# Decoder layer on one core: sixteen W2 product banks and eleven transposes moved from ScalarE to VectorE, and norms laid in other places

## The chip, the cores and the metric

The kernel runs on one core of a Trainium2 chip. The metric is the device time of one execution in microseconds (us), and a kernel is told by the median of several runs. The engines are TensorE (PE, with its weight loads PEld), VectorE (DVE), ScalarE (ACT), GpSimd (POOL) and SyncE (SP), which issues most transfers. Each engine works through its own instructions in a fixed order; an instruction that waits for another engine holds up all that stand behind it.

## The reference

One decoder layer in float32 on x of 16 x 112 x 512 (1792 tokens), with a context of 16 x 375 x 512 and its mask. D = 512, 16 heads of 32, a hidden width of 2048:

```python
x = x + self_attention(layernorm(x))        # q, k, v low-rank: Wdown, Wup fold into the weights
x = x + cross_attention(layernorm(x), ctx, mask)
      # clip(scores) -> softmax -> @ v -> Wo + bo; delta = rs * that;
      # delta is normalised again, times ln_gamma plus ln_beta
x = x + ffn(layernorm(x))
      # hidden = silu(x W1^T) * (x W3^T); hidden = fwht(hidden); hidden @ W2^T
```

The Hadamard transform `fwht` of the hidden vector (2048 wide, over sqrt(2048)) is applied by the kernel to W2 instead.

## The kernel before, in words

The 1792 tokens are 14 tiles of 128 rows (`xr`) and also 16 batches of 112 tokens; 4 batches make a group. `xyT` holds the tokens transposed, as input of every projection. PSUM has three banks named `mm`, which projections, transposes and W2 products share in turn; `sc` (two pairs of banks) takes scores and transposes of the exponentials; `ys` takes the weighted values.

**PE's order is written out by hand.** Every piece of PE work that has slack is a generator that yields the microseconds it took, and `Filler` draws from a queue of such pieces between the steps of attention: `fill(us)` draws that much, `drain()` the rest. `mixed(a, b, skip)` draws `skip` pieces from `a` and then one of each in turn. A new piece takes the `mm` bank that comes free first; its matmuls wait for the copy that empties that bank. The other engines' instructions are ordered by a scheduler, around the instruction that `tc.issue_after` names.

**Start.** The layer norm of the first tiles (`n1[0]`), the folded weights (`fold`, L849 to L857), the first group's queries and keys. Then `attention.begin` puts out the first scores, and behind them the fold of wv is mixed with the transposes of `n1[1]` (L1622 to L1625).

**Self attention** goes through 16 lays, one for each batch. Lay b (`SelfAttention.step`, L1002) first issues the scores of batch b + 1: on DVE two maxima (L981) and their scaling (L982), then on ACT 16 exponentials (L986), 8 for each half; then on DVE sum, reciprocal and multiply for each half (L997 to L999). While these run, PE fills with the lay's pieces: queries or keys of the next group (L865, copied out of PSUM by ACT at L871), values (L883, copied at L888), transposes of normalised tiles (L826, copied by ACT at L827), W2 products, or the output projection (L894). Then PE transposes the exponentials of batch b (L1019, copied by ACT at L1021) and multiplies them with the values (L921).

**W2** is transformed in two parts. In lays 0 to 3 PE multiplies it with a Hadamard matrix, four products a lay (L1539), and ACT copies each bank back with a factor (L1542). From lay 1 on, `w2_steps` does the rest on DVE and ACT: subtraction and addition (L1569, L1570) and a copy (L1571), 4 or 5 steps a lay (`prepared`), put behind the lay's last multiply. Its last steps store blocks to DRAM from row buffers; rows of one kind (`row`) share four buffers with `xn`.

**Norms.** `Norm.start` does statistics (L766, L767), a reciprocal root by 12 small instructions (`rstd_of`, L774 to L786), and a normalised row tile `xn` for each token tile (L792). `n1` norms feed the self projections, `n2` the cross projections, `n3` the feed-forward part. Before, `n1[2]` is started ahead of lay 2, `n1[3]` ahead of lay 7, and each `n2[g]` at the end of `after_self`, the self output projection of group g, in lays 5, 9, 12 and in cross batch 0.

**Cross attention** goes through 16 batches with three key blocks each (`Cross.step`). For each block: scores, exponentials (L1244) and a check pass (L1248) on ACT, weighted values of the block before (L921), and on DVE the addition of the exponentials (L1274). At a batch's end `divide` sums over keys (L932), takes four reciprocals (L1284) and multiplies (L1285). PE fills with values, keys and queries of the next batch: values are copied by DVE (L888), the keys' sums of products are made on DVE (L1110 to L1143, and L1054 which reads the context `cT` straight from a load). In batches 3, 7 and 11 the next group's transposes are mixed with its queries. `AfterCross` does the cross output projection of a group, then its own norm and the residual (`finish`: rstd, L1202, L1210, statistics), then starts `n3`. `pieces()` runs `finish` as one burst behind the projections.

**Feed-forward** (`Pass`) follows, bound by PE.

Of the kernel before, what the change touches and what calls it, by code (L numbers as in the profile page):

```python
# [14 lines left out]
AF = mybir.ActivationFunctionType  # L15
# [3 lines left out]
P = 128  # L19
# [578 lines left out]
def finite_layer(  # L598
# [203 lines left out]
    class Norm:  # L802
# [11 lines left out]
                normalised(self.l, self.tiles, self.rstd, k) for k in range(len(self.tiles))  # L814
            ]

        def begin(self):
            self.start(True)
            yield 0.0

        def transposes(self):

            for k, t in enumerate(self.tiles):
                tr = psum("mm", [P, C, P])
                for c in range(C):
                    nc.tensor.transpose(tr[:, c, :], self.xn[k][:, ts(c, P)], ident)  # L826
                nc.scalar.copy(xyT[:, :, ts(t, P)], tr)  # L827
                yield 0.5
            if self.l == 1:

                beta = row("beta")
                nc.gpsimd.dma_start(out=beta, in_=c_beta.partition_broadcast(P))
                for t in self.tiles:
                    nc.gpsimd.tensor_tensor(xr[:, t, :], xr[:, t, :], beta, ALU.add)
# [124 lines left out]
    def after_self(tiles, norm):  # L959

        for t in tiles:
            yield from project(
                wo, t, lambda acc: nc.vector.tensor_tensor(xr[:, t, :], acc, xr[:, t, :], ALU.add)
            )
            stats(xr[:, t, :], norm.l, t)
        norm.start(False)

    class SelfAttention:


        def begin(self, b, grp):
            bl = b % GB
            scs = scores(
                lambda i, j: grp.q[ds(i * DH, DH), j, ts(bl, S)],
                lambda i, j: grp.k[ds(i * DH, DH), j, ts(bl, S)],
                S,
            )
            es = []
            for sc, (tag, bufs) in zip(scs, (("q", 2), ("es", 3))):
                mx = ln.tile([S, 2, HG], F32, tag="mx", name="mx")  # L980
                nc.vector.reduce_max(mx, sc, axis=AX.X)  # L981
                nc.vector.tensor_scalar(mx, mx, -SCALE, None, op0=ALU.mult)  # L982
                e = pair("e", tag, bufs)[:S]
                for i in range(2):
                    for j in range(HG):
                        nc.scalar.activation(  # L986
                            e[:, i, j, :],
                            sc[:, i, j, :],
                            AF.Exp,
                            scale=SCALE,  # L990
                            bias=mx[:, i, j : j + 1],
                        )
                es.append((e, mx))


            for e, total in es:
                nc.vector.reduce_sum(total, e, axis=AX.X)  # L997
                nc.vector.reciprocal(total, total)
                self.behind = nc.vector.tensor_tensor(  # L999
                    e, e, total.unsqueeze(3).to_broadcast([S, 2, HG, S]), ALU.mult  # L1000
                )
            self.next = b, grp.v, [e for e, _ in es]  # L1002
# [177 lines left out]
    class AfterCross:  # L1180
# [15 lines left out]
        def finish(self):  # L1196

            rstd = rstd_of(2, self.tiles, rs2)
            nc.vector.tensor_scalar(rstd, rstd, rs, None, op0=ALU.mult)
            for k, t in enumerate(self.tiles):  # L1200
                d = self.d[k]
                nc.vector.scalar_tensor_tensor(  # L1202
                    d,
                    in0=d,
                    scalar=mv[:, 2, t, 0:1],
                    in1=rows["gamma"],
                    op0=ALU.subtract,
                    op1=ALU.mult,
                )
                nc.vector.scalar_tensor_tensor(  # L1210
                    xr[:, t, :],
                    in0=d,
                    scalar=rstd[:, k : k + 1],
                    in1=xr[:, t, :],
                    op0=ALU.mult,
                    op1=ALU.add,
                )
                stats(xr[:, t, :], self.norm.l, t)
            self.norm.start(False)

        def pieces(self):
            yield from self.projections()
            self.finish()

    class Cross:

# [44 lines left out]
        def add(self, late, i):  # L1271
            if late is not None and late[1] > 0:
                total = self.es[i][:KP]
                nc.vector.tensor_tensor(total, total, late[3][i][:KP], ALU.add)  # L1274

        def divide(self, late):
            if late is not None and late[1] == KC - 1:
# [258 lines left out]
    def w2_products(h, w):  # L1536
        for c in range(0, UNITS, 2):
            acc = psum("mm", [P, D])
            nc.tensor.matmul(  # L1539
                acc, h, w[:, ds(c, 2)].rearrange("p c n -> p (c n)"), start=True, stop=True  # L1540
            )
            nc.scalar.activation(  # L1542
                w[:, ds(c, 2)].rearrange("p c n -> p (c n)"),
                acc,
                AF.Copy,
                scale=1.0 / math.sqrt(FF),
            )
            yield 0.9

# [50 lines left out]

    pe = ctx.enter_context(tc.manual_schedule(engines={mybir.EngineType.PE}))
    f = Filler()

    n1 = [Norm(0, r) for r in read]
    n2 = [Norm(1, r) for r in whole]
# [12 lines left out]
    f.drain()  # L1618
    n1[1].start(True)
    f.add(mixed(grp[0].keys(), block_products(1)))  # L1620
    f.drain()
    attention = SelfAttention()  # L1622
    attention.begin(0, grp[0])
    f.add(mixed(fold(wv, raws[2], bdm[1]), n1[1].transposes()), grp[0].values(range(GB)))
    f.drain()  # L1625
    w2_load()
    h = w2_matrix()
# [4 lines left out]
    def lay(b, us, *pieces, prepared=0):  # L1632
        f.add(*pieces)
        attention.step(b, grp[min(b + 1, B - 1) // GB], f, us, prepared)

    lay(0, 15.5, mixed(grp[1].queries(), w2_products(h, w2[0])))
    lay(1, 15.5, mixed(grp[1].keys(), w2_products(h, w2[1])), prepared=4)
    n1[2].start(True)
    lay(2, 14, mixed(grp[1].values(range(3)), w2_products(h, w2[2])), prepared=4)
    lay(  # L1640
        3,
        9.5,
        mixed(grp[1].values(range(3, GB)), w2_products(h, w2[3])),
        n1[2].transposes(),
        prepared=4,
    )

    lay(4, 12, grp[2].queries(), prepared=4)
    lay(5, 10.5, after_self(whole[0], n2[0]))
    lay(6, 13.5, mixed(grp[2].keys(), n2[0].transposes(), 5), prepared=5)  # L1650
    n1[3].start(True)
    lay(7, 15.5, mixed(grp[2].values(range(GB)), n1[3].transposes(), 3), prepared=5)

    lay(8, 12, grp[3].queries(), prepared=5)
    lay(9, 14, after_self(whole[1], n2[1]))
    lay(10, 14, mixed(grp[3].keys(), n2[1].transposes(), 5), prepared=5)
    for _ in w2_prep:
        pass
    xk, xv, xq, xo = (weight(n) for n in ("xk", "xv", "xq", "xo"))
# [2 lines left out]
    load_weight(xq, c_wq_t)  # L1662
    load_weight(xo, c_wo_t)
    kv.append(Keys(0))
    lay(11, 14, grp[3].values(range(GB)))

    xks = weight("xks").rearrange("p c n -> p (c n)").rearrange(
        "p (s k n) -> p s k n", s=4, k=2
# [3 lines left out]
    ]  # L1672
    s_sums(xks, *xk_blocks)
    lay(12, 10.5, after_self(whole[2], n2[2]))
    lay(13, 10, kv[0].first_keys())
    kv.append(Keys(1))
    lay(14, 12, mixed(kv[0].values(), n2[2].transposes(), 3))
    qs = [Queries(n) for n in range(B // 2)]
# [2 lines left out]
    cross = Cross()  # L1681
    n3w = None
    passes = [Pass(n) for n in range(2)]
    for b in range(B):
        g, bl = divmod(b, GB)
        us = 0.0
        if b + 2 < B:
            kv.append(Keys(b + 2))
        if b + 1 < B:
            kv[b + 1].sums()  # L1690
            us += 19.5
        if bl == 0:
            if g == 0:
                f.add(after_self(whole[3], n2[3]))
            elif g < 3:
                f.add(AfterCross(whole[g - 1], n3[g - 1]).pieces())
            us += 13.0 if g < 3 else 0.0
        if b + 1 < B:


            f.add(mixed(kv[b + 1].values(), kv[b + 1].keys(), 2))
            if b % 2:
                queries = qs[(b + 1) // 2].pieces()
                us += 6.0
                if bl == 3 and g < 3:
                    queries = mixed(queries, (n2[3] if g == 0 else n3[g - 1]).transposes())
                    us += 2.0
                f.add(queries)
        if b == B - 1:
            after = [AfterCross(whole[g], n3[g]) for g in (2, 3)]  # L1710
            f.add(after[0].projections())
            us += 10.5
        if b == B - 2:
            ready.update({(0, i): load_blocks(0, i) for i in range(2)})
        if b == B - 1:
            passes[0].token_sums()
        for kc in range(KC):
            cross.step(b, kc, qs[b // 2].q, kv[b], f, us / KC)
        f.drain()
    cross.weigh(cross.late)  # L1720
    cross.add(cross.late, 0)
# [27 lines left out]
    p.start()  # L1749
    p.products(0, 0)  # L1750
    with tc.issue_after(p.last):
        after[0].finish()
    p.products(0, 1)
    def tiles_of(pieces):

        for _ in pieces:
            next(pieces, None)
            yield

    def tiles_of(pieces):  # L1760
# [5 lines left out]
    late = itertools.chain(  # L1766
        itertools.repeat(None, 1),
        n3[2].transposes(),
        tiles_of(after[1].pieces()),
        itertools.repeat(None, 3),  # L1770
        n3[3].transposes(),
    )
# [97 lines left out]
```

## Time and profile before

| | us |
|---|---|
| runs of the kernel before: lowest, median, highest | 1395.64, 1396.09, 1397.08 |
| the profiled execution | 1396.93 |
| its span (first to last instruction) | 1395.1 |
| DVE busy, ACT busy in the span | 785.2, 470.7 |
| idle of PE at 52.53, ended by ACT's copy of wv (L857) | 3.05 |
| idle of PE at 76.94, 98.49, 121.70, 140.84, ended by ACT's W2 copy (L1542) | 1.95, 1.97, 1.53, 1.53 |
| idle of PE at 155.50 and 307.98, ended by exponentials (L986) | 1.28, 2.65 |
| idle of PE at 473.00, 609.22, 746.44, ended by ACT's copy of transposes (L827) | 1.32 each |
| idle of PE at 505.66, 645.77, ended by DVE's copy of values (L888) | 2.17, 1.09 |

Times at the left are where the idle time ends, counted from the span's start. The profile is of one execution: its own time is 1.83 us longer than its span, and 0.84 above the median of the runs. In the profile a row names line, engine and operation, the tiles written and read, and how long; `<-` in brackets names the engine and line that ended the wait ahead of it. "Granted clock" is the share of TensorE's full clock that the chip gave in a stretch of time.

### The profile page before, as it was taken

How to read it: one execution, taken by the hardware profiler on the slowest of the kernel's cores; microseconds unless marked ns; L12 is line 12 of the kernel's file. 1: busy time of each engine (PE TensorE's matmuls, PEld its weight loads, DVE VectorE, ACT ScalarE, POOL GpSimd, SP SyncE). 2: the span in 40 equal slices, each digit the busy share in tenths (PEclk: the TensorE clock that was granted, in tenths of full speed). 3: DMA queues.
4: the chain of work that ended last, by engine and by line, in shares of the span. 5: the costliest groups of instructions: out<-in, count | busy, mean ns of one | idle time of the engine just before them, and what ended most of it. 6: DMA issues, size and time to landing. Idle time of an engine off the chain costs nothing.

```text
span 1395.1 us, 20037 instructions
## 1 busy us (share of the span) xinstructions
PE 1357.1 (97%) x8328; PEld 809.2 (58%) x8328; DVE 785.2 (56%) x1493; ACT 470.7 (34%) x917; POOL 36.5 (3%) x68
## 2 busy tenths in 40 slices
PE   8989999999999999999999999999999999999997
PEld 5544555556676757666777775544555555555554
DVE  5244998773646575558554556756754235555332
ACT  3355755544244434443445355110110001111000
POOL 2000010030000100000000000000000000000000
PEclk9999999999999999999999999999999999999999
DMA  9100002421000000000000102111031112311301
GB/s 322 42 1 0 31 8 84 166 90 46 23 23 24 30 24 23 24 23 23 23 24 23 39 16 61 46 46 46 20 123 59 56 59 84 91 61 66 115 1 55
DMA packets 59719, 74.02 MB, mean 53 GB/s; under 512 B 2640, under 2 KB 47712, under 8 KB 57316
## 3 DMA queue, kind: packets, MB, share of 16 engines
q1 hardware_dynamic: 57952, 69.44, 15.0%
q0 software_dynamic: 672, 1.62, 0.4%
q8 instruction: 67, 1.10, 0.3%
q10 hardware_dynamic: 996, 1.59, 0.3%
q14 instruction: 32, 0.26, 0.1%
HBM read 61.63 MB, written 11.01 MB: 52 GB/s over the span
## 4 chain that ended last, share of the span: by engine, by line
PE 85%; DVE 9%; ACT 4%; issue 1%; DMA 1%; POOL 0%; SPq 0%; ACTq 0%; DVEq 0%; POOLq 0%
PE mm L883 13%; PE gate L1454 12%; PE mm L1096 9%; PE mm L865 8%; PE ys L1454 7%; PE mm L894 6%; PE gate L1388 6%; PE mm L1454 5%; PE sc L910 4%; PE ys L1388 3%; PE ys L921 3%; PE mm L1388 3%; ACT e L986 2%; DVE mx L981 1%; PE sc L1019 1%
## 5 line engine op out<-in xcount | busy, mean ns | idle before, releaser
L883 PE MATMUL mm<-xv,cT 128*125 128x512 f32 x384 | 180.4, 606 | 3.3 <-DVE v L888 3.3
L1244 ACT ACTIVATE e<-sc,bia,scl 125x896 f32<-125x896 f32 x64 | 68.5, 1095 | 200.3 <-PE sc L910 200.3
L883 PEld LDWEIGHTS mm<-xv,cT 128*125 128x125 f32 x384 | 68.7, 188 | 79.7 <-issue 74.7
L1248 ACT ACTIVATE sc<-sc,limit,nscl 125x896 f32<-125x896 f32 x96 | 102.7, 1070 | 0.0
L1454 PE MATMUL gate<-t,f 128*128 128x448 f32 x256 | 101.4, 539 | 0.0
L1274 DVE TENSOR_TENSOR es<-es,e 125x896 f32<-125x896 f32 x64 | 68.4, 1089 | 47.3 <-ACT e L1244 47.3
L1388 PE MATMUL gate<-h,f 128*128 128x448 f32 x224 | 86.6, 539 | 0.0
L1454 PE MATMUL gate<-xyT,f 128*128 128x448 f32 x192 | 80.1, 540 | 0.0
L986 ACT ACTIVATE e<-sc,mx 112x112 f32<-112x112 f32 x256 | 64.6, 400 | 44.8 <-DVE mx L982 44.7
L1454 PE MATMUL ys<-t,f 128*128 128x448 f32 x192 | 77.4, 539 | 0.0
L1454 PEld LDWEIGHTS gate<-t,f 128*128 128x128 f32 x256 | 48.6, 190 | 47.6 <-issue 47.0
L1284 DVE RECIPROCAL r<-mm 128x112 f32<-128x112 f32 x64 | 47.9, 810 | 39.8 <-PE mm L932 39.8
L1470 ACT COPY u<-gate 128x448 f32<-128x448 f32 x16 | 8.5, 531 | 182.3 <-PE gate L1454 109.4
L1096 PEld LDWEIGHTS mm<-kt,xks 128*128 128x128 f32 x360 | 59.0, 190 | 15.3 <-issue 14.8
L981 DVE TENSOR_REDUCE mx<-sc 112x8 f32<-112x896 f32 x32 | 33.5, 1084 | 59.5 <-PE sc L910 59.5
L1388 PEld LDWEIGHTS gate<-h,f 128*128 128x128 f32 x224 | 42.5, 190 | 41.3 <-issue 40.9
L1096 PE MATMUL mm<-kt,xks 128*128 128x188 f32 x360 | 63.5, 324 | 0.0
L883 PE MATMUL mm<-wv,xyT 128*112 128x512 f32 x128 | 58.1, 598 | 2.0 <-ACT w L1542 1.5
L1454 PEld LDWEIGHTS ys<-t,f 128*128 128x128 f32 x192 | 36.5, 190 | 35.7 <-issue 35.5
L865 PE MATMUL mm<-xyT,xq 128*128 128x224 f32 x256 | 52.5, 356 | 4.2 <-ACT xyT L827 4.0
L1454 PEld LDWEIGHTS gate<-xyT,f 128*128 128x128 f32 x192 | 36.0, 190 | 34.4 <-issue 33.7
L1400 DVE TENSOR_TENSOR h<-h,h 128x896 f32<-128x896 f32 x32 | 32.8, 1087 | 40.9 <-PE ys L1388 31.6
(211 smaller groups left out, 2212.7 us busy)
## 6 DMA issues: line engine op xcount, KB each, us to landing
f<-in_f_w SPq DMA_DIRECT2D x64, 256.0 KB, 3.1
f<-blocks SPq DMA_DIRECT2D x14, 1024.0 KB, 4.8
cT<-in_ctx SPq DMA_DIRECT2D x16, 750.0 KB, 4.8
w<-in_f_w SPq DMA_DIRECT2D x4, 1024.0 KB, 10.3
blocks<-w SPq DMA_DIRECT2D x4, 1024.0 KB, 4.8
xr<-in_x SPq DMA_DIRECT2D x2, 1024.0 KB, 10.8
out_y<-o SPq DMA_DIRECT2D x8, 256.0 KB, 3.2
xr<-in_x SPq DMA_DIRECT2D x2, 768.0 KB, 15.8
```

The lines of the kernel that those rows point to most:

```text
L865: nc.tensor.matmul(acc[:, :n], w[:, c, ts(j, P)], src[:, c, :], start=(c == 0), stop=(c == C - 1))
L883: nc.tensor.matmul(acc[:n, :], src[:, c, :], w[:, c, :], start=(c == 0), stop=(c == C - 1))
L894: nc.tensor.matmul(acc, xyT[:, c, ts(t, P)], w[:, c, :], start=(c == 0), stop=(c == C - 1))
L910: nc.tensor.matmul(views[i // 2][:, i % 2, j, :], k_of(i, j), q_of(i, j), start=True, stop=True)
L986: nc.scalar.activation(e[:, i, j, :], sc[:, i, j, :], AF.Exp, scale=SCALE, bias=mx[:, i, j : j + 1],)
L1096: nc.tensor.matmul(acc[:, m], lhs[:, k, ts(m, P)], rhs[:, k], start=first and m == 0 and k == 0, stop=k == 1, skip_group_check=True,)
L1244: nc.scalar.activation(es[i], sc, AF.Exp, scale=scl[:, n : n + 1], bias=bia[:, n : n + 1])
L1248: nc.scalar.activation(sc, sc, AF.Relu, scale=nscl[:, n : n + 1], bias=limit[:KP, :1], accum_out=low[:KP, 2 * n + i : 2 * n + i + 1],)
L1274: nc.vector.tensor_tensor(total, total, late[3][i][:KP], ALU.add)
L1284: nc.vector.reciprocal(r[:, c], sums[:, c])
L1388: nc.tensor.matmul(banks[m][bank], o[:, c, ts(m, P)], t[:, c, :], start=first and c == 0, stop=c == UNITS - 1, skip_group_check=True,)
L1454: nc.tensor.matmul(bank, o[:, s, k, :], t[:, k, :], start=first and k == 0, stop=k == 1, skip_group_check=True,)
```

## The change

- The 16 banks of W2 products are copied out of PSUM by DVE (`tensor_scalar` with the factor) instead of ACT.
- The transposes of `n2[3]`, `n3[0]` and `n3[1]` in cross batches 3, 7 and 11 (eleven tiles) are copied by DVE instead of ACT.
- The fold of wv and the transposes of `n1[1]` come ahead of the first scores.
- `Norm.ahead` puts a norm behind the scaled maxima of a lay: `n1[2]` in lay 1, `n1[3]` in lay 4, `n2[0]`, `n2[1]`, `n2[2]` in lays 6, 10 and 13. Their transposes are mixed into other lays: `n1[2]` with the values and W2 products of lay 3, `n1[3]` with the output projection in lay 5, `n2[0]` and `n2[1]` with the values in lays 7 and 11. The budgets of lays 5, 6, 7, 10 and 11 change.
- `AfterCross.finish` and the norms behind it yield after each tile, and two such pieces are put behind the last addition of each key block, in the three later batches of a group. `n2[3]` is laid in the same way.

```diff
+        def ahead(self, with_stats):
+            with tc.issue_after(attention.maxed):
+                self.start(with_stats)
             yield 0.0
-        def transposes(self):
+        def steps(self):
+            self.rstd, self.xn = rstd_of(self.l, self.tiles), []
+            yield 0.0
+            for k in range(len(self.tiles)):
+                self.xn.append(normalised(self.l, self.tiles, self.rstd, k))
+                yield 0.0
+        def transposes(self, copy=nc.scalar.copy):
...
-                nc.scalar.copy(xyT[:, :, ts(t, P)], tr)
+                copy(xyT[:, :, ts(t, P)], tr)
...
-        norm.start(False)
...
-                nc.vector.tensor_scalar(mx, mx, -SCALE, None, op0=ALU.mult)
+                self.maxed = nc.vector.tensor_scalar(mx, mx, -SCALE, None, op0=ALU.mult).ins
...
             rstd = rstd_of(2, self.tiles, rs2)
             nc.vector.tensor_scalar(rstd, rstd, rs, None, op0=ALU.mult)
+            yield 0.0
             for k, t in enumerate(self.tiles):
...
                 stats(xr[:, t, :], self.norm.l, t)
-            self.norm.start(False)
+                yield 0.0
+            yield from self.norm.steps()
...
-            nc.scalar.activation(
+            nc.vector.tensor_scalar(
                 w[:, ds(c, 2)].rearrange("p c n -> p (c n)"),
                 acc,
-                AF.Copy,
-                scale=1.0 / math.sqrt(FF),
+                1.0 / math.sqrt(FF),
+                None,
+                op0=ALU.mult,
             )
...
+    f.add(mixed(fold(wv, raws[2], bdm[1]), n1[1].transposes()))
     f.drain()
-    attention = SelfAttention()
     attention.begin(0, grp[0])
-    f.add(mixed(fold(wv, raws[2], bdm[1]), n1[1].transposes()), grp[0].values(range(GB)))
+    f.add(grp[0].values(range(GB)))
...
-    lay(1, 15.5, mixed(grp[1].keys(), w2_products(h, w2[1])), prepared=4)
-    n1[2].start(True)
+    lay(1, 15.5, n1[2].ahead(True), mixed(grp[1].keys(), w2_products(h, w2[1])), prepared=4)
...
-        mixed(grp[1].values(range(3, GB)), w2_products(h, w2[3])),
-        n1[2].transposes(),
+        mixed(
+            mixed(grp[1].values(range(3, GB)), n1[2].transposes()), w2_products(h, w2[3])
+        ),
...
-    lay(4, 12, grp[2].queries(), prepared=4)
-    lay(5, 10.5, after_self(whole[0], n2[0]))
-    lay(6, 13.5, mixed(grp[2].keys(), n2[0].transposes(), 5), prepared=5)
-    n1[3].start(True)
-    lay(7, 15.5, mixed(grp[2].values(range(GB)), n1[3].transposes(), 3), prepared=5)
+    lay(4, 12, n1[3].ahead(True), grp[2].queries(), prepared=4)
+    lay(5, 12.5, mixed(after_self(whole[0], n2[0]), n1[3].transposes(), 1))
+    lay(6, 12, n2[0].ahead(False), grp[2].keys(), prepared=5)
+    lay(7, 15.5, mixed(grp[2].values(range(GB)), n2[0].transposes(), 1), prepared=5)
...
-    lay(10, 14, mixed(grp[3].keys(), n2[1].transposes(), 5), prepared=5)
+    lay(10, 12, n2[1].ahead(False), grp[3].keys(), prepared=5)
...
-    lay(11, 14, grp[3].values(range(GB)))
+    lay(11, 15.5, mixed(grp[3].values(range(GB)), n2[1].transposes(), 1))
...
-    lay(13, 10, kv[0].first_keys())
+    lay(13, 10, n2[2].ahead(False), kv[0].first_keys())
...
-                    queries = mixed(queries, (n2[3] if g == 0 else n3[g - 1]).transposes())
+                    n = n2[3] if g == 0 else n3[g - 1]
+                    queries = mixed(queries, n.transposes(nc.vector.tensor_copy))
...
             cross.step(b, kc, qs[b // 2].q, kv[b], f, us / KC)
+            if bl > 0:
+                with tc.issue_after(cross.last):
+                    for _ in range(2):
+                        next(finish, None)
```

More of the change, by code (lines that the diff above doesn't have):

```diff
@@ L815, in start @@
             ]
-        def begin(self):
-            self.start(True)
+        def ahead(self, with_stats):
+            with tc.issue_after(attention.maxed):
+                self.start(with_stats)
             yield 0.0
-        def transposes(self):
+        def steps(self):
[5 more added lines that the diff above has]
+        def transposes(self, copy=nc.scalar.copy):
             for k, t in enumerate(self.tiles):
@@ L1218, in finish @@
                 stats(xr[:, t, :], self.norm.l, t)
-            self.norm.start(False)
-        def pieces(self):
-            yield from self.projections()
-            self.finish()
+                yield 0.0
+            yield from self.norm.steps()
     class Cross:
@@ L1273, in add @@
                 total = self.es[i][:KP]
-                nc.vector.tensor_tensor(total, total, late[3][i][:KP], ALU.add)
+                self.last = nc.vector.tensor_tensor(
+                    total, total, late[3][i][:KP], ALU.add
+                ).ins
         def divide(self, late):
@@ L1602, in finite_layer @@
     f = Filler()
+    attention = SelfAttention()
     n1 = [Norm(0, r) for r in read]
@@ L1636, in finite_layer @@
     lay(0, 15.5, mixed(grp[1].queries(), w2_products(h, w2[0])))
-    lay(1, 15.5, mixed(grp[1].keys(), w2_products(h, w2[1])), prepared=4)
-    n1[2].start(True)
+    lay(
+        1,
+        15.5,
+        n1[2].ahead(True),
+        mixed(grp[1].keys(), w2_products(h, w2[1])),
+        prepared=4,
+    )
     lay(2, 14, mixed(grp[1].values(range(3)), w2_products(h, w2[2])), prepared=4)
@@ L1683, in finite_layer @@
     passes = [Pass(n) for n in range(2)]
+    finish = iter(())
     for b in range(B):
@@ L1694, in finite_layer @@
                 f.add(after_self(whole[3], n2[3]))
+                finish = n2[3].steps()
             elif g < 3:
-                f.add(AfterCross(whole[g - 1], n3[g - 1]).pieces())
+                c = AfterCross(whole[g - 1], n3[g - 1])
+                f.add(c.projections())
+                finish = c.finish()
             us += 13.0 if g < 3 else 0.0
@@ L1751, in finite_layer, with at_once @@
     with tc.issue_after(p.last):
-        after[0].finish()
+        run(after[0].finish())
     p.products(0, 1)
+    def at_once(pieces):
+        run(pieces)
+        yield from ()
     def tiles_of(pieces):
@@ L1768, in finite_layer @@
         n3[2].transposes(),
-        tiles_of(after[1].pieces()),
+        tiles_of(after[1].projections()),
+        at_once(after[1].finish()),
         itertools.repeat(None, 3),
```

## The prediction

> **What bounds the kernel now.** I read the page's busy row and chain first, then the list of what TensorE (PE) waited for, then a table of windows with the granted clock, last the timelines around single waits.
>
> ```profile
> PE 1357.1 (97%) x8328; PEld 809.2 (58%) x8328; DVE 785.2 (56%) x1493; ACT 470.7 (34%) x917; POOL 36.5 (3%) x68
> ...
> PE 85%; DVE 9%; ACT 4%; issue 1%; DMA 1%; POOL 0%; SPq 0%; ACTq 0%; DVEq 0%; POOLq 0%
> ```
>
> PE is busy 1357.1 of 1395.1 us: only its idle 38 us, and any loss of clock, can be moved. The change does not shorten PE's work. Where is the 38?
>
> ```profile
> PE mm L865 <- ACT xyT L827: 4.6, 4, 1.3
> PE sc L1019 <- ACT e L986: 4.2, 3, 2.6
> PE mm L865 <- ACT w L1542: 3.9, 2, 2.0
> PE mm L883 <- DVE v L888: 3.3, 2, 2.2
> PE mm L826 <- ACT wv L857: 3.0, 1, 3.0
> ...
> PE mm L883 <- ACT w L1542: 1.5, 1, 1.5
> PE mm L1539 <- ACT w L1542: 1.5, 1, 1.5
> PE mm L1096 <- DVE kT L1133: 1.2, 2, 0.9
> ```
>
> Columns: total us, times, longest. These eight rows are what the change aims at: W2 copies (6.9), cross transposes (3.96 of the 4.6), the burst of the cross finish (2.17 + 1.09 + 0.89), the wv fold (3.05), a norm burst ahead of the maxima (2.65 of the 4.2).
>
> A stall costs more than its length when it drops the clock:
>
> ```profile
> 96.20:99.62 3.42, 1.45 (x4) 0.68 (x4) 3.31 (x5) 3.16 (x11) 0.00 (x0) 1.00 0.00 0
> 99.62:103.03 3.41, 3.41 (x9) 1.64 (x8) 3.38 (x6) 0.52 (x1) 0.00 (x0) 0.50 0.00 0
> ...
> 502.39:505.80 3.41, 1.24 (x8) 0.95 (x8) 3.27 (x14) 0.00 (x0) 0.00 (x0) 1.00 0.00 0
> 505.80:509.21 3.41, 3.41 (x5) 1.32 (x6) 2.63 (x10) 0.00 (x0) 0.00 (x0) 0.50 0.00 0
> ```
>
> Columns: length, busy us of PE, PEld, DVE, ACT, POOL, then the clock. Windows in which PE idled 1.97 to 2.5 us are followed by 3.41 us at clock 0.50; windows with 1.53 us idle are not. Four such halved windows lie ahead of the tail (from 51.83, 99.62, 307.83, 505.80), and each loses half of what PE does in it: 2.71/2 = 1.35 for the first, about 3.3/2 = 1.65 for the others. The Trainium skill (TensorE: Matmul & The Clock Gate, Part 1: The HAM clock gate) has the half rate come after at least one idle window of about 3.4 us; here 1.97 us inside a window was enough, so the measurement decides. By the page's rule every clock term below would go, and the sum would be +0.55 instead of +1.6.
>
> **Part by part.** I walked PE, DVE and ACT in the issue order of the changed program, with durations from rows of before: W2 product 0.86, four transposes 0.45, value half-product 0.86, 16 exps 4.03, maxima pair 2.09 + 0.29, sum, reciprocal and multiply 2.37 a half, PSUM copies 0.59 on ACT (L827) and 0.69 on DVE (L888, pitch 0.62), W2 step operation 0.62.
>
> *Start.* The wv fold and n1[1]'s transposes come ahead of the first scores, so their bank copies no longer queue behind the first 16 exps on ACT. Gap 3.05 and the 1.35 of clock go: −4.4. Floor of the gain 3.05. Nothing is late next, as ACT idles there.
>
> *Self lays.* ACT loses 16 W2 copies, DVE gains 16 × 0.62 = 9.9 us. DVE's FIFO then has, behind one lay's maxima, step operations, copies and sums, and its next maxima wait behind those.
> - Lays 0 to 2: idle of 1.95 + 1.97 + 1.53 = 5.45 becomes 0 + 0.7 + 1.2 = 1.9. What is left are qT, kT and v copies on ACT behind exps.
> - Lay 3 (scores end at 133.9 in before's time). n2's transposes now lie among the W2 products. PE does half a v product, transposes 0, W2 product 1, half a v product: done 136.95. Transposes 1 take the bank of W2 copy 1, which DVE reaches behind maxima (136.3) and two step operations: 138.2, a wait of 1.3. W2 product 2 takes the bank of transposes 0, copied on ACT behind 16 exps and one step's copy: 136.26 + 4.03 + 0.5 + 0.6 = 141.4, PE was there at 138.7: 2.7. With 0.5 at product 4, and 0.6 in lay 4 (its maxima stand behind the last steps and copies), lays 3 and 4 cost 5.1 to 5.3 where 1.53 + 1.28 = 2.81 stood.
> - Lays 5 to 7: 0.74 becomes 3.85. Lay 5: n1[3]'s statistics, rstd (12 × 0.2) and four xn (1.9) keep DVE behind its maxima (1.2). Lay 7: transposes 1 reuse the bank of v0, whose ACT copy stands behind 16 exps (1.3), and the maxima come 1.6 late behind n2[0]'s norm: 2.65.
> - Lays 8 to 10: 0.24 becomes 0. Lay 11: as lay 7, 2.7; and the four xn wait on DVE for row buffers from which W2 blocks are being stored, behind a 1-MB store, with the split maxima queued behind them: 2.0 more. 4.7 in all, the least certain figure (bounds 0 and 9).
> - Lay 13: n2[2]'s norm goes behind the maxima, 2.65 goes. Lay 15 keeps 0.73.
>
> Sum: 12.6 becomes 16.5, +3.9. Bounds: −8 if DVE always has a gap when a copy falls due, +10 if each late maxima pair delays its lay in full.
>
> *Cross transposes* (b = 3, 7, 11): three copies of four transposes move to DVE.
>
> ```profile
> 472.04 1.01 DVE L1054 TENSOR_TENSOR kt<-cT 128x376 f32<-128x376 f32 x2 [1.59 <-DMA cT<-in_ctx]
> ...
> 472.36 0.59 ACT L827 COPY xyT<-mm 128x512 f32<-128x512 f32 x1
> ...
> 473.00 1.02 PE L865 MATMUL mm<-xyT,xq 128*128 128x224 f32 x4 [1.32 <-ACT xyT L827]
> ```
>
> In the new order the first copy stands on DVE behind two L1054, which wait for a context load that lands at 472.04. So it runs at 472.04 + 0.93 and ends near 473.6, where ACT's copy released PE at 473.0: stalls of 2.02, 2.47, 2.03 for 1.32 each, +2.55. Bounds: −3.96 if the load lands before it is wanted, +4.
>
> *Cross finish in pieces.* The bursts of rstd and xn ahead of v copies are spread behind the additions: 2.17 + 1.09 + 0.89 = 4.15 goes. Late next is the division: behind the additions of b = 4 and 8 DVE now has rstd 13 × 0.2, three L1202 (0.66), two L1210 (0.66) besides its four L1054, and the reciprocals (2.99) end 2.6 later than at 525.8; the sums' bank is wanted at 527.9, so 0.65 each, +1.3. Bounds 0 and 3.8.
>
> *At nothing.* SP issues the same 79 transfers, a few block stores in another order; POOL and the feed-forward part keep their work and order.
>
> *Clock.* Three trips go (−5.0). New stalls of 2.0 to 2.7 us trip it only if they fall mostly inside one 3.41 us window: (3.41 − 2.0 + 0.5)/3.41 = 0.57 for the 2.0, 0.7 for the 2.5 to 2.7 (lays 3, 7, one cross), surely for lay 11. With lay 4 in doubt about 4.5 trips × 1.65 = 7.4: net +2.4 (bounds −5 and +7).
>
> All: −4.4 + 3.9 + 2.55 − 4.15 + 1.3 + 2.4 = **+1.6** on the profiled execution's 1396.93 (span 1395.1 and 1.83 around it): 1398.5. That execution lies 0.84 above the runs' median of 1396.09, so the forecast is 1397.7, put at 1398.
>
> **Rivals.**
> 1. *Clean gain.* DVE idles 44% of the span, and if it reaches every copy in time, all the idle aimed at goes: 4.4 + 6.98 + 2.65 + 3.96 + 4.15 and three trips of 1.65 = 27, so 1369; with half of the new idle left (11 us and two trips), 1383. For it: in lays 0 to 2 DVE is busy 16 of 35 us. Against it: strict order in lays 3 to 7 (DVE 32 of 35 us busy from 140 to 210).
> 2. *DVE becomes the bound of the lays (slower).* In lays 3 to 5, 7 and 11 the maxima wait for the queue of copies, steps and xn, exps and e-transposes follow, and each trips the clock. It decides once maxima are more than about 1.8 us late, the time PE has work without them (before, lay 4's came at 151.08, 3.1 after the scores, and that cost 1.28). Price: my 16.5 becomes 22 and the trips 7: +5.5 + 4.1, 1407.
> 3. *Stores hold lay 11 only.* Without the 2.0 and one trip the forecast falls to 1394; with 9 us it rises to 1402.
>
> **Chances.** Forecast case (1392 to 1403, the third rival in it) 0.48; clean 0.26; slower rival 0.26. The 80% range takes in the half-clean case and the second rival: 1383 to 1409. A measurement here tells about 0.2% (2.8 us) from no change: faster is below 1393.3, slower above 1398.9. The clean case and 0.08 of the forecast case are faster (0.34), 0.24 same, the rest slower (0.42).
>
> **What would show it.** Right: no PE wait on L857 at the start nor on W2 copies in lay 0; waits of PE on DVE's copies or on ACT's transposes copies in lay 3; PE waiting for DVE's transposes copies after the context load at b = 3, 7, 11; no wait on v near b = 4 and 8, but a short one at the reciprocals; halved windows in lays 7 and 11. Wrong: PE's idle total below 25 us (rival 1), or L981 over 2 us behind its scores in several lays with e-transposes waiting on exps (rival 2).

## The result, and the profile after

| | median us | runs | lowest to highest |
|---|---|---|---|
| before | 1395.88 | 10 | 1393.77 to 1399.04 |
| changed | 1391.36 | 10 | 1389.64 to 1393.31 |

The ratio is 0.9967, 95% interval 0.9956 to 0.9977: the changed kernel is 4.5 us (0.33%) faster. The forecast was 1398; the time lies inside its range, on the other side of "no change". The profiled execution took 1390.56 us (span 1388.8), 0.8 below its median, as before's lay 0.84 above its own, so the two spans differ by 6.3 us.

The busy row and the chain of the changed kernel:

```profile
PE 1355.0 (98%) x8328; PEld 808.2 (58%) x8328; DVE 796.1 (57%) x1520; ACT 457.5 (33%) x890; POOL 37.1 (3%) x68
...
PE 86%; DVE 7%; DMA 2%; ACT 2%; issue 1%; POOL 0%; SPq 0%; ACTq 0%; POOLq 0%; DVEq 0%
```

DVE took 11 us more, ACT 13 us less. The chain that ends last now runs through transfers for 2% of the span, where it was 1%. What PE waits for (columns: total us, times, longest):

```profile
PE mm L874 <- DVE xyT L836: 6.5, 3, 2.2
PE mm L835 <- ACT v L897: 5.5, 2, 3.4
...
PE sc L1027 <- ACT e L994: 2.7, 2, 1.9
PE mm L1547 <- ACT xyT L836: 2.0, 1, 2.0
PE mm L1104 <- DVE r L1292: 1.1, 2, 0.7
```

(Lines of the changed kernel: L836 copies transposes, L897 values, L994 is the exponential, L1292 the reciprocal, L1547 the W2 product.) Five of the eight rows shown of before are gone: the W2 copies, the wv fold, the value copies of the cross finish. Four new ones stand in their place, each foretold by its cause: cross transposes on DVE, a value bank in lays 7 and 11, a transpose bank in lay 3, reciprocals behind the finish.

A sum over the trace shows where the time went. I add up PE's idle gaps over 0.06 us, and half of PE's busy time in each window at clock 0.50 ahead of the tail (a halved window), and call what is left of the span "work":

| kernel | span | idle gaps | halved windows, their loss | work |
|---|---|---|---|---|
| before | 1395.1 | 31.2 | 4, 6.4 | 1357.4 |
| changed | 1388.8 | 26.7 | 3, 5.1 | 1356.9 |

Idle fell 4.5 us and the clock's loss 1.3, in these two executions; work stayed. By places, the idle of the changed kernel against before's:
- start: 3.05 gone;
- lays 0 to 2: 0, 0.40, 0 for 1.95, 1.97, 1.53;
- lays 3 and 4: 2.02 and 1.88 for 1.53 and 1.28;
- lays 5 to 13: 0.79 (lay 5), 2.11 (lay 7), 3.36 (lay 11) for 0.74, 0.24 and 2.65;
- cross transposes: 2.17, 2.14, 2.17 for 1.32 each;
- cross finish: 2.17, 1.09 and 0.89 gone, 0.44 and 0.69 at the reciprocals and 0.6 more in batch 0 new.

Lay 3 shows a wait in full. First PE, then ACT of the changed kernel (start, length, what):

```profile
125.33 1.88 PE L892 MATMUL mm<-wv,xyT 128*112 128x512 f32 x4
127.05 0.60 PE L835 MATMUL mm<-ident,xn 128*128 128x128 f32 x4
129.66 1.13 PE L1547 MATMUL mm<-w,bd 128*128 128x512 f32 x2 [2.02 <-ACT xyT L836]
```

```profile
124.59 2.07 ACT L994 ACTIVATE e<-sc,mx 112x112 f32<-112x112 f32 x8 [2.68 <-DVE mx L990]
126.50 0.67 ACT L1580 COPY w<-diff 128x512 f32<-128x512 f32 x1
127.00 2.13 ACT L994 ACTIVATE e<-sc,mx 112x112 f32<-112x112 f32 x8
128.91 0.70 ACT L836 COPY xyT<-mm 128x512 f32<-128x512 f32 x1
```

The W2 product needs the bank of the first transposes; ACT could copy it at 124.6, but has 16 exponentials and a step's copy ahead of it in its queue, until 128.9.

### The profile page after: what moved, and what is told of

The parts are those of the page before. It is cut to its first block, busy times and chain, and to the rows that moved or that the text cites. A ratio compares the mean times of both kernels' runs of the same rounds, so it can differ in the third digit from the quotient of the medians.

```text
span 1388.8 us, 20028 instructions
## 1 busy us (share of the span) xinstructions
PE 1355.0 (98%) x8328; PEld 808.2 (58%) x8328; DVE 796.1 (57%) x1520; ACT 457.5 (33%) x890; POOL 37.1 (3%) x68
## 3 DMA queue, kind: packets, MB, share of 16 engines
q10 hardware_dynamic: 996, 1.59, 0.3%
## 4 chain that ended last, share of the span: by engine, by line
PE 86%; DVE 7%; DMA 2%; ACT 2%; issue 1%; POOL 0%; SPq 0%; ACTq 0%; POOLq 0%; DVEq 0%
PE mm L892 14%; PE gate L1462 12%; PE mm L1104 9%; PE mm L874 8%; PE ys L1462 7%; PE mm L903 7%; PE gate L1396 6%; PE mm L1462 5%; PE sc L919 4%; PE ys L1396 3%; PE ys L930 3%; PE mm L1396 3%; PE sc L1027 1%; DMA cT<-in_ctx 1%; ACT e L994 1%; PE mm L835 1%
## 5 line engine op out<-in xcount | busy, mean ns | idle before, releaser
L994 ACT ACTIVATE e<-sc,mx 112x112 f32<-112x112 f32 x256 | 64.7, 403 | 45.4 <-DVE mx L990 45.4
L1292 DVE RECIPROCAL r<-mm 128x112 f32<-128x112 f32 x64 | 47.8, 809 | 31.2 <-PE mm L941 31.2
```

Of the source, the lines that this page charges most:

```text
L994: nc.scalar.activation(e[:, i, j, :], sc[:, i, j, :], AF.Exp, scale=SCALE, bias=mx[:, i, j : j + 1],)
L1292: nc.vector.reciprocal(r[:, c], sums[:, c])
```

## The experiments

Medians of all runs (us); before was measured beside each group at 1395.3 to 1396.3, the changed kernel beside the first pair alone. A ratio below is to the before of its own group, with its 95% interval. The intervals are 0.001 to 0.002 wide on either side, so a difference from the changed kernel's 1391.36 is good to about 2 us.

| run | what differs from the changed kernel | median | idle gaps | halved |
|---|---|---|---|---|
| u_start | start as before | 1395.18 | 28.3 | 6 |
| u_w2 | W2 copies on ACT | 1396.52 | 30.3 | 5 |
| u_finish | cross finish in a burst | 1396.22 | 29.0 | 6 |
| u_cross | cross transposes on ACT | 1387.68 | 24.8 | 3 |
| u_norms | self norms as before | 1385.96 | 24.0 | 3 |
| f_skip3 | transposes of lays 7, 11 two pieces later | 1382.24 | 21.4 | 3 |
| f_lay3 | order of lay 3 as before | 1392.83 | 26.6 | 5 |
| f_dum_mm | matmuls that nobody reads in lays 3, 7, 11 | 1392.25 | 23.9 | 1 |
| f_dum_tr | transposes that nobody reads there | 1392.41 | 23.8 | 1 |
| f_cross_dum | u_cross with the matmuls of f_dum_mm | 1384.86 | 19.5 | 0 |
| f_comb2 | the winning parts alone | 1376.90 | 16.7 | 0 |
| f_comb3 | and cross transposes later | 1372.14 | 13.9 | 1 |

Idle gaps and halved windows are those of the one profiled execution. In every row span less idle less the clock's loss is 1355 to 1358, or 1363 with the added matmuls and transposes (about 5.9 us of them).

### One part undone at a time

u_cross: `n.transposes(nc.vector.tensor_copy)` becomes `n.transposes()`.

> The changed kernel with the eleven cross transposes copied by ACT again. Theory A (a part is worth the PE idle it puts in or takes out, plus about 1.65 us for each halved window): the three stalls of 2.17, 2.14 and 2.17 us at batches 3, 7 and 11 become 1.32 each, -2.5 us, and the halved window behind batch 3 goes, -1.65: 1387 to 1389. Rival B (ACT, freed of the copies, was what let the exponentials of these batches come in time): no gain or a loss, 1391 to 1393.

1387.68 against 1391.36, ratio to before 0.9944 (0.9931 to 0.9957). The three stalls are 1.32 each again. The halved window behind batch 3 is gone; the profile has one behind lay 7 in its place. Why a copy on DVE comes later than on ACT shows in DVE's timeline of the changed kernel:

```profile
463.34 1.09 DVE L1280 TENSOR_TENSOR es<-es,e 125x896 f32<-125x896 f32 x1 [1.65 <-ACT e L1250]
466.17 1.01 DVE L1062 TENSOR_TENSOR kt<-cT 128x376 f32<-128x376 f32 x2 [1.74 <-DMA cT<-in_ctx]
467.10 0.68 DVE L836 COPY xyT<-mm 128x512 f32<-128x512 f32 x1
```

DVE has nothing to do from 464.43 to 466.17, with the bank full: the copy stands behind a subtraction (L1062) that waits for a context load. Theory A holds, rival B falls.

u_w2: the `tensor_scalar` at L1550 becomes the `activation` of before.

> The changed kernel with the 16 W2 product banks copied by ACT again. Theory A: the idle of 1.5 to 2 us in each of lays 0 to 2 comes back (+5), lay 3 stalls longer since both its copies stand behind the exponentials on ACT (+0 to +2), lay 4's 1.88 shrinks towards 0.6 as DVE has 2.5 us less ahead of its maxima, one or two more halved windows: 1395 to 1399. Rival B (DVE's load is what the lays wait for, so copies cost on DVE what they cost on ACT): 1390 to 1392.

1396.52, ratio 1.0002 (0.9992 to 1.0011): the W2 copies on DVE are worth 5.2 us. The list of PE's waits in this run has the idle back almost to the digit:

```profile
PE mm L874 <- ACT w L1550: 3.9, 2, 2.0
PE mm L835 <- ACT xyT L836: 3.3, 2, 2.5
...
PE mm L892 <- ACT w L1550: 1.5, 1, 1.5
```

and lay 4's 1.88 fell below 0.2, as the copies no longer stand ahead of its maxima: these start 1.45 us behind their scores, 3.78 in the changed kernel. So DVE's load does cost, but about 2 us in lay 4 against 5 gained in lays 0 to 2, 0.8 in lay 3 and two halved windows: rival B falls as a whole and holds for lay 4.

u_finish: `finish` runs at the end of the projections again, and the norm of `n2[3]` at the end of its own.

> The changed kernel with the cross finish and the norms behind it in one burst again. Theory A: idle of 2.17 + 1.09 + 0.89 at the values comes back, 0.44 + 0.69 at the reciprocals and 0.6 of 0.93 at batch 0 go: +2.4, and a halved window near batch 4, +1.65: 1394 to 1396. Rival: the burst was covered anyway and the pieces changed nothing, 1391 to 1392.

1396.22, ratio 0.9990 (0.9976 to 1.0003): 4.9 us, a little over the expected 4.1. Idle of 2.11, 1.09 and 0.90 is back; the profile has three halved windows more.

u_start:

```diff
-    f.add(mixed(fold(wv, raws[2], bdm[1]), n1[1].transposes()))
     f.drain()
     attention.begin(0, grp[0])
-    f.add(grp[0].values(range(GB)))
+    f.add(mixed(fold(wv, raws[2], bdm[1]), n1[1].transposes()), grp[0].values(range(GB)))
```

> The changed kernel with the fold of wv and the transposes of n1[1] behind the first scores again. Theory A: the idle of 3.05 us and the halved window behind it (1.35) come back: +4.4, about 1395.5. Rival: the later lays have slack that takes it up, 1391 to 1393.

1395.18, ratio 0.9990 (0.9976 to 1.0003): 3.8 us, with a gap of 3.04 and a halved window behind it in the trace. The idle gaps together rose by 1.6 only: lay 5's 0.79 went, and 0.6 of batch 0's 0.93.

u_norms: `n1[2]`, `n1[3]` and the `n2` norms start where they started before, their transposes and the budgets of lays 1 to 13 as before; W2 copies stay on DVE.

> The changed kernel with the self norms and their transposes where they were before (lays 1 to 13 as before, W2 copies still on DVE). Theory A: the idle of 2.02, 1.88, 0.79, 2.11 and 3.36 in lays 3, 4, 5, 7 and 11 and two halved windows (3.3) go, about 0 to 1.5 in lays 3 and 4, 0.28 + 0.38 + 0.24 and 2.65 in lay 13 with its halved window come back: -2 to -6, 1385 to 1389. Rival C (laying the norms behind the maxima is what made the change faster): 1395 or more.

1385.96, ratio 0.9928 (0.9915 to 0.9941). The re-laying of the norms **cost** 5.4 us. Without it lays 5 and 11 have no gap and lay 3 only 0.56; lay 4 has 2.21, lay 7 1.36, lay 13 2.87 with two halved windows behind it. So lay 13's part of the re-laying is a gain, and the rest costs more than the 5.4. Rival C falls.

The five parts add up: 3.8 + 5.2 + 4.9 won, 3.7 + 5.4 lost, net 4.8 won, where the whole change measured 4.5. By the ratios the net is 2.7; with 2 us of doubt on each part, the close agreement of the medians is partly luck. The signs are clear: the change is three gains with two losses inside it.

### Why the re-laid norms lose

f_skip3: in lays 7 and 11 `mixed(..., n2[g].transposes(), 1)` becomes `3`.

> The changed kernel with the transposes of lays 7 and 11 mixed in behind three value half-products instead of one. Theory A (they wait for the bank of the first value product, whose copy stands on ACT behind 16 exponentials): PE has 1.72 us more work ahead of the first claim on that bank, so 2.11 becomes about 0.4 and 3.36 about 1.7, and lay 11's halved window goes: -3.4 to -5, 1386 to 1388. Rival C (they wait because xn and the maxima come late behind the transfers of W2 blocks): the stalls stay, 1390 to 1392.

1382.24, ratio 0.9907 (0.9888 to 0.9925): 9.1 us faster, about twice the expected. The gap of lay 7 went and lay 11 kept 0.90 where 1.7 was expected, as eight transposes of exponentials (0.77 us) also came ahead of the claim: 4.6 us of idle less. The mechanism (the bank of the first value product, behind 16 exponentials) holds. Rival C falls as the whole cause; in lay 11 it is part of it, since the maxima start 2.4 us late in both kernels. The rest is the clock: the mean granted clock of its runs has a median of 0.997, that of the changed kernel's 0.994, and one halved window in 1390 us takes 0.0012, so some 2.5 windows less, 4.1 us (an estimate from clocks that are given to 0.001). (The execution that was profiled lies 2.3 us above its median.) I had counted one. Lay 11 in the changed kernel, first DVE, then ACT:

```profile
259.53 1.15 DVE L792 TENSOR_SCALAR xn<-xr,seen,rstd 128x512 f32<-128x512 f32 x2 [1.59 <-DMA blocks<-g]
260.60 1.08 DVE L989 TENSOR_REDUCE mx<-sc 112x8 f32<-112x896 f32 x1
261.60 1.00 DVE L792 TENSOR_SCALAR xn<-xr,seen,rstd 128x512 f32<-128x512 f32 x2
```

```profile
262.76 4.03 ACT L994 ACTIVATE e<-sc,mx 112x112 f32<-112x112 f32 x16 [4.95 <-DVE mx L990]
266.57 0.70 ACT L897 COPY v<-mm 112x512 f32<-112x512 f32 x1
```

The scores end near 258.2; `xn` waits for a W2 block to leave its row buffer, so the maxima come 2.4 us late, the exponentials start at 262.8, and the value bank that PE wants at 264.0 is copied at 266.6.

f_lay3: lay 3's pieces as before, `mixed(values, w2_products)` and then `n1[2].transposes()`.

> The changed kernel with lay 3's pieces in the order of before: values and W2 products first, then n1[2]'s transposes. Theory A: the 2.02 us there (W2 product 2 waits for the bank of transposes 0, copied by ACT behind 16 exponentials) becomes about 0.6 as in the run with the old norms; the 1.88 of lay 4 stays or grows to 2.2: -1 to -1.5, with one halved window less in some runs -1.65 more: 1388.5 to 1390.5. Rival (W2 copies on DVE are what lay 3 waits for): 2 us stay, 1391 to 1392.

1392.83, ratio 0.9977 (0.9965 to 0.9988): not faster, a miss. Lay 3 fell to 0.56 and lay 4 grew to 2.21 as foretold, so its rival falls too. But on DVE the last of `n1[3]`'s twelve small instructions ended 5.4 us behind the scores of lay 5, 1.4 in the changed kernel, and PE waited there for `xn`, as the list of its waits has it:

```profile
PE mm L835 <- DVE xn L792: 2.4, 1, 2.4
```

where the changed kernel waits 0.79 in lay 5, for exponentials. I had looked at two lays only; what they saved on DVE's queue was lost in the third. Why the small instructions came so much later is not shown.

### What a halved window costs

f_dum_mm puts matmuls of the identity, which nobody reads, into PE's order in lays 3, 7 and 11, where PE waits; f_dum_tr puts transposes there.

```diff
+    def extra(n):
+        o = psum("ys", [P, C, S]).rearrange("p c s -> p (c s)")[:, :P]
+        for _ in range(n):
+            nc.tensor.matmul(o, ident, ident, start=True, stop=True)
...
+                if k == 1 and self in (n2[0], n2[1]):
+                    extra(12 if self is n2[1] else 7)
                 tr = psum("mm", [P, C, P])
...
+                if k == 1 and self is n1[2]:
+                    extra(7)
```

> The changed kernel with matmuls of the identity that nobody reads, put in PE's order where it waits: 7 in lay 3 and in lay 7 (about 1.5 us), 12 in lay 11 (2.6 us); nothing else is changed. Theory A for the clock (idle of about 1.8 us and more inside one window halves the next): the halved windows behind lays 3, 7 and 11 go, the times at which the stalls end stay, -1.65 for each that a run would have had, on average two: 1387 to 1389. Rival D (only a window idle from end to end counts, and the halved windows have another cause): no gain, 1391 to 1393.

> The same with transposes in place of the matmuls: 14 in lays 3 and 7, 24 in lay 11, of about the same length. If transposes count as work for the clock as matmuls do: as with the matmuls, 1387 to 1389. If they don't: halved windows behind these lays as in the changed kernel, 1391 to 1393.

1392.25 and 1392.41: no gain, though the halved windows behind these lays were gone in both profiles, and lay 15's gap came 3.1 and 2.8 us sooner than in the changed kernel. With the matmuls, 2.4 of the 3.1 us were lost again in cross attention: the stall of batch 3 was 2.98 where it had been 2.17, with 0.42 more behind it, since the context load that DVE waits for took 5.8 us from issue to use (458.2 to 464.0) where it took 5.0 (461.2 to 466.2); and the last key product waited 1.47 for 0.28, behind a weight load. So waits for loads, of the kind that u_cross had shown, took most of the gain.

What delayed the context load shows in the list of transfers from 457 to 467 us of f_dum_mm (packets, MB, share of the DMA engines; then size and us to landing):

```profile
q8 instruction: 1, 0.02, 0.6%
cT<-in_ctx SPq DMA_DIRECT2D x1, 750.0 KB, 5.7
```

One packet of the queue that the list calls instruction, 16 KB in 0.95 us, runs while the load does. The three kernels with added matmuls or transposes have it in the load of batch 3, which lands 5.70 to 5.77 us after its issue; in the other eleven profiles no such packet falls into that load, and it lands in 4.75 to 5.03. No run moves that packet alone, so this is the likely cause and not a shown one. Why the medians of the two kernels lie 1.7 and 2.6 us above their profiled executions is not settled. The test again, with the copies on ACT:

> The changed kernel with the cross transposes on ACT and with the identity matmuls in the stalls of lays 3, 7 and 11. The first run with these matmuls lost two of its three halved windows but not its time: 3 us of idle came up in cross attention, where DVE waits for context and weight loads. If that was the loads' doing and a halved window costs about 1.65 us: against the run with cross transposes on ACT (1387.7, three halved windows in its profile) two to three windows less, 1383 to 1385, and no idle over 1.4 us from batch 3 on. Rival D (a halved window costs nothing here that the idle ahead of it does not): 1387 to 1388.5.

1384.86 (1384.68 to 1385.52), ratio 0.9924 (0.9910 to 0.9938), against 1387.68 (1387.15 to 1388.38) without the matmuls: 2.8 us, no halved window in its profile, the cross stalls at 1.32. Here are the windows around lay 11 (length, busy us of PE, PEld, DVE, ACT, POOL, the clock, the DMA share and GB/s), first of the changed kernel, then with the matmuls:

```profile
264.23:267.64 3.41, 0.32 (x3) 0.32 (x4) 2.71 (x4) 3.41 (x13) 0.00 (x0) 1.00 0.98 291
267.64:271.06 3.42, 3.42 (x8) 1.49 (x6) 3.35 (x6) 0.70 (x2) 0.00 (x0) 0.50 0.95 293
```

```profile
263.00:266.40 3.40, 2.69 (x25) 2.50 (x24) 2.67 (x4) 3.40 (x13) 0.00 (x0) 1.00 0.98 286
266.40:269.80 3.40, 3.40 (x21) 2.26 (x20) 3.33 (x6) 1.82 (x5) 0.00 (x0) 1.00 1.01 300
```

The wait ends at the same instruction, but PE then runs at full clock. Rival D falls. Of the 5.1 us that the three windows cost in u_cross's profile 2.8 were won by the medians (3.5 by the spans); 1.2 went to two key products that waited 1.07 and 1.01 for 0.60 and 0.27, and 0.4 by the spans, 1.1 by the medians, is not accounted for.

### The best version

f_comb2: start, W2 copies and cross finish as changed; cross transposes on ACT; lays 1 to 12 as before, `n2[2].ahead` in lay 13 as changed; `prepared` 0 in lay 2, 2 each in lays 5 and 9.

> The parts that won and none of those that lost: start, W2 copies on DVE and cross finish as changed; cross transposes on ACT and the self norms of lays 1 to 12 as before; n2[2] behind the maxima of lay 13 as changed; and the four W2 steps of lay 2 moved to lays 5 and 9, two each. Theory A: against the run with the old self norms (1386.0): cross -2.6, lay 13's 2.87 with its halved windows -4.5, lay 4's 2.21 shrinks by 1 to 2: 1375 to 1380. Rival B (DVE's load is the limit, so steps moved to lays 5 and 9 stall there): 1381 to 1385.

1376.90, ratio 0.9868 (0.9848 to 0.9889), as expected; lay 13 has no gap, lay 4 1.08.

f_comb3: the kernel of f_comb2 with `mixed(queries, n.transposes(), 6)` in the cross batches.

> The best version so far (1376.9) with the cross transposes, on ACT, mixed in behind six pieces of the queries. Theory A: PE has three more pieces of 0.9 us ahead of the first claim on the first transposes' bank, which ACT copies behind the two check passes: the three stalls of 1.32 go, -3.9, 1373. Rival (the banks of the query products, which ACT copies behind the same passes, are waited for in their place): 1376 to 1377.

1372.14, ratio 0.9833 (0.9815 to 0.9851): the three stalls are gone. This was expected; it is 19 us below the changed kernel. What is left in its list of PE's waits is small; the first rows:

```profile
PE sc L1622 <- POOL ident masks.py:199: 2.9, 1, 2.9
PE sc L1027 <- ACT e L994: 1.7, 3, 1.1
PE mm L892 <- ACT v L897: 1.5, 1, 1.5
```

## Why the prediction was wrong, point by point

Two rows of PE's timeline of before, from lay 3, bear on the step that failed. They are half a product of values and what PE starts next:

```profile
133.90 1.97 PE L883 MATMUL mm<-wv,xyT 128*112 128x512 f32 x4
135.71 1.02 PE L1539 MATMUL mm<-w,bd 128*128 128x512 f32 x2
```

- **Start** (−4.4): right in the trace (3.05 of idle and its window); undone alone it cost 3.8.
- **Cross transposes** (stalls 2.02, 2.47, 2.03): 2.17, 2.14, 2.17; +2.55 foretold, +2.52 measured, for the reason given; that the sum is so close is luck, as the second was 0.33 shorter and the others 0.15 longer than foretold. Undone alone, 3.7 came back.
- **Cross finish** (−4.15, then +1.3 at the reciprocals): −4.15 and +1.13 (0.44 and 0.69 for 0.65 each). Missed: the pieces of `n2[3]` in batch 0 add 0.6.
- **Self lays** (16.5 us of idle where 12.6 stood): **this is the step that failed.** They came to 11.3 us, so −1.3 instead of +3.9, 5.2 of the 7.9 us by which the sum missed the profiled span. All the places but three were right (the wait of lay 2 and two of lay 3 did not come), and nearly every size was too large, lay 4's alone too small. Lay 3 (4.5 foretold, 2.02 measured): I took a half-product of values at 0.86; it is four matmuls in the profile and takes 1.72 (from 125.33 to 127.05 in the changed kernel's lay 3). The two rows of before above have it too, 1.81 from one start to the next. With 1.72 for each half the prediction's own walk brings PE to the second transposes at 138.7, behind the copy that ends at 138.2, and to the next W2 product at 139.1, 2.3 ahead of 141.4. So the 1.3 was no wait at all, and the 2.7 was 2.02. Lay 4 cost more than foretold, 1.88 for 0.6: its maxima start 3.78 us behind the scores. Lay 2 (1.2 foretold): the maxima were to be late behind DVE's backlog; the backlog ended at 105.08, 0.1 us behind the scores. Lay 1 was 0.40 for 0.7, lay 5 0.79 for 1.2, lay 7 2.11 for 2.65 with maxima 1.06 us late where 1.6 were assumed, lay 11 3.36 for 4.7 with maxima 2.4 us late where 3.6 (1.6 and 2.0) were assumed. The walk added each full duration end to end, where DVE's small instructions, when they stand between large ones, add 0.1 us rather than 0.2.
- **Clock** (+2.4 net of three windows lost, beside the 1.35 of the start): in the two profiled executions 4 halved windows became 3, −1.3 in all where +1.05 was foretold; the stalls of 2.1 in lay 7 and at batches 7 and 11 tripped nothing. But these two executions are not typical. Before's was granted a clock of 0.993, where its runs in the three later groups average 0.9943 to 0.9947; the changed kernel's was granted 0.995, the highest of its ten runs, which average 0.9936. As 0.001 is 1.4 us, the changed kernel lost 1 to 1.5 us more to the clock than before, over all these runs: the forecast of this term was about right, and so were its price (1.35 to 1.7) and its mechanism.
- **The sum**: idle +0.55 foretold, −4.5 measured. The working had the wrong sign for the self lays and so for the total, because a gain of 8.6 us and a loss of 10.2 stood against each other, and 5.2 of the loss, idle in the lays, did not come (in the two profiled executions 2.3 of clock as well). All the signs of being right came but the halved window of lay 7; they named places, not sizes, and the error was in sizes.
- **At nothing**: the trace has 134 transfers issued by SP in both kernels, not 79; that their number does not change was right.
- **Rival 1** (clean gain): half of it. The W2 copies on DVE were nearly clean; in lays 0 to 2 its condition, DVE free when a copy falls due, held. **Rival 2** (DVE as the bound): its condition, maxima more than 1.8 us late, held in lays 4, 5 and 11 alone (3.78, 2.83 and 2.40). **Rival 3** (stores in lay 11): the wait is there, 1.59 us long.

## What to carry to other kernels

A change made of several moves is read one move at a time: here three gains of 14 us carried two losses of 9, and undoing either loss alone took the gain from 4.5 us to 8 or 10. Before a copy is moved to an idler engine, look at what stands ahead of it in that engine's queue at the moment when it falls due: DVE was idle for 1.7 us with the cross copy ready, and could not take it because the instruction in front waited for a load. When PE waits for one of several banks in turn, move the first claim on a late bank back by one or two pieces (9 us for one number changed in two places) before moving work between engines.

## What the runs showed of the hardware

**When the clock is halved.** Over the fourteen profiles (before, changed and twelve runs) I cut each execution, from 12 us to the tail, into windows of 3.413 us on the grid of its own halved windows and added up PE's idle time in each. Of the windows at full clock, every one with 1.99 us of idle or more was followed by a halved one; none with less than 1.64 was; between 1.64 and 1.99 both occurred (1.73 to 1.985 without, 1.64 and 1.78 to 1.97 with). The grid lies elsewhere in each execution, so that a stall of 2 us falls inside one window or is shared by two: the 2.02 us of lay 3, the same in five kernels within 0.01, was followed by a halved window in three of the profiles. That is one reason why runs of the kernel before spread from 1391.8 (granted clock 0.997) to 1403.0 (0.990). A window that was halved already stayed so with 0.8 to 1.3 us of idle (four cases); with 0.7 or less it did not. The Trainium skill (TensorE: Matmul & The Clock Gate, Part 1: The HAM clock gate) asks for an idle window of about 3.4 us; these rows halve the clock at 2.

**Transposes keep the clock up.** With 24 transposes in lay 11 in place of 12 matmuls the next window stayed at 1.00 as well, although the window of the wait would have held 2.83 us of idle without them. The Trainium skill (TensorE: Matmul & The Clock Gate, Part 4: PE-mode transpose) says that transposes do not count as busy in the same way; here, in float32, no difference showed.

**A packet of instructions goes with a slower load.** The context load of batch 3, 750 KB and alone on its queue, took 4.8 to 5.1 us to its use in eleven profiles and 5.8 to 5.9 in the three in which an instruction packet of 16 KB fell into it. Kernels with the copies on DVE behind such loads had stalls of 1.79 to 2.98 us at batches 3, 7 and 11, those with the copies on ACT in the order of before 1.31 to 1.32 in every profile.
